# A graph-network layer on one core: the order of GpSimd's gathers written out by hand, in groups of 9, 9 and 6 behind points of TensorE

## The chip, the cores and the metric

The kernel runs on one core of a Trainium2 chip. The metric is device time in microseconds (us) of one execution. Before the change the median of three runs is 3001.91 us (3001.52 to 3004.13). A profiled execution, taken apart from these, took 2999.86 us; the span of its trace, from the first to the last instruction, is 2998.0 us.

The engines are named as the profile names them: PE is TensorE's matrix products and PEld its weight loads, DVE is VectorE, ACT is ScalarE, POOL is GpSimd, SP is SyncE, which only issues DMAs here.

## The reference

One layer of message passing over 12,500 nodes and 400,000 edges, which are sorted by their target `dst`. Each edge looks up the normalised features of its source and its target, passes a small two-layer network, and each node takes the maximum over the edges that end in it.

```python
h = jnp.maximum(_layernorm(x, axis=-1), 0.0)          # [12500, 32]
e_feat = jnp.concatenate([h[src], h[dst], edge_attr_32], axis=-1)
v = jax.nn.relu(e_feat @ W1 + b1) @ W2 + b2           # [400000, 96] -> 64 -> 32
x_cand = jax.ops.segment_max(v, dst, num_segments=num_nodes)
return x + jnp.maximum(x_cand, h[:, -32:])
```

## The kernel before

**Tiling.** The 400,000 edges are cut into four stripes, which lie side by side on 4 x 32 partitions. A stripe is walked in 196 chunks (`NCH`) of 512 edges (`C`), so a chunk is 4 x 512 edges. The main loop (L560) takes two chunks at a time: its counter c goes 0, 2, 4, and so on, and the iteration c finishes the chunks c and c + 1 and prepares the pair a = c + 2 and b = c + 3, for the most part.

**Where the source's features come from.** A chunk needs 16 columns (`K`) of 128 source rows. Twelve are fetched: GpSimd issues one indirect DMA for a column, 128 rows of 32 floats out of the table `h_d` in DRAM (`gather`, L153 to 162, the DMA itself at L159). Three columns (`SOME`) share one tile `gh`, here called a part: a chunk has 4 parts and a pair 8, that is 24 gathers. The parts are counted through from 0 for the pair 2, 3; the tile pool `gathered` has 18 buffers for them (L91). The other four columns (`MM`) are not fetched but multiplied out: `tile` (L245) has TensorE multiply a one-hot matrix `hot` with the table `hs` that lies in SBUF, 14 products of 128 x 448 into a PSUM bank `pv` (L256), and VectorE picks the row out of it (L260, L261). PSUM has three `pv` buffers, and other steps of the loop take them in turn too. The first two chunks have no such columns and are fetched from `x` itself (`raw_gather`, L168, 32 gathers in four calls `raw_gather(0)` to `(3)` with three buffers `xg`, so that the fourth waits for the first one's reader at L361); the last chunk has none either.

**From rows to features.** `to_features(c, part)` (L263) has VectorE transpose one part of `gh` into the chunk's tile `ht` (L274), or, with part = 4 (`J`), the result of `tile` (L277). VectorE works in order: the transposition of a part that has not landed holds up all that stands behind it.

**One iteration**, in TensorE's order: `into_ph` with `w1a` and the `ht` of the chunks c and c + 1 (16 products into four `ph` banks, L527), the transposition of the previous pair's result (`leave_1`, L500), `tile(a, 1)`, `edges_into(a)` (L527 with `ea`), the second layer (L586 into two `pv` banks), `windows_into(a)` (L527 with `qw`), `leave_2` (L511), and then a stretch of seven tiles without a break: `tile(a, 2)`, `tile(a, 3)`, `tile(b, 0)` to `tile(b, 3)`, `tile(a + 2, 0)`. VectorE follows with the same tiles' rows, with the parts between them (`to_features`), with its share of the one-hot matrices (L225) and with a scan (L594). In iteration c = 182 alone a check of the input stands behind `to_features(a + 2, 0)`: five small steps of VectorE and a product of TensorE at L637.

**Loads.** Every second iteration brings in four chunks' edge features, targets and penalties (`load`, L461): 1 MB through SP's queue and 1.5 MB through ScalarE's.

**What sets the order.** SP, PE, DVE and ACT run their instructions in the order of the source (`manual_schedule`, L180). GpSimd is left to the scheduler, which places the gathers that the source calls for in one go per chunk (L554 and L618). Its program: small constants, `raw_gather(0)` to `(2)`, the first ten gathers of `gh`, `raw_gather(3)`, the other 2,311 gathers, one addition (`again`, L621), which reuses the memory of the gathers' indices and so stands behind all of them. Its result is read in the last stage (L730). A gather waits for one made eight gathers before, and the first one of a part also for the reader of the buffer's last contents.

Of the kernel before, what the change touches and what calls it, by code (L numbers as in the profile page):

```python
# [11 lines left out]
BF16 = mybir.dt.bfloat16  # L12
I32 = mybir.dt.int32
AF = mybir.ActivationFunctionType
ALU = mybir.AluOpType
# [3 lines left out]
SP = mybir.EngineType.SP  # L19
PE = mybir.EngineType.PE  # L20
DVE = mybir.EngineType.DVE
ACT = mybir.EngineType.Activation

P = 128
N = 12500
E = 400000
D = 32
# [6 lines left out]
J = C // P  # L34
K = C // D
HALF = K // 2
NCH = 196
# [7 lines left out]
A0 = NT // A1  # L45
MM = 4
MMC = range(2, NCH - 1)
SOME = 3
# [3 lines left out]
FIRST = 16  # L52
PIECE = 2 * A0
GP = 3
ROUND = 12582912.0
LOW = 1e30
BY_ACT = range(A1 - 2, A1)
# [10 lines left out]
def gnn_kernel(ctx, tc, x, src, src_mm, src_t, dst, dst_ext, lo, lo_c, ends_b, edge_attr, weights, w1, w2, b2, out):  # L68
# [19 lines left out]
    nc = tc.nc  # L88
    const = ctx.enter_context(tc.tile_pool(name="const", bufs=1))
    dram = ctx.enter_context(tc.tile_pool(name="dram", bufs=1, space=DRAM))  # L90
    gathered = ctx.enter_context(tc.tile_pool(name="gathered", bufs=18))  # L91

    h_d = dram.tile([NP, D], F32, name="h_d")
    q_d = dram.tile([NP, HID], F32, name="q_d")
# [11 lines left out]
    pieces = [slice(k, min(k + PIECE, NT)) for k in range(0, NT, PIECE)]  # L106
    nc.scalar.dma_start(xs[:, pieces[GP]], x_v[:, pieces[GP]])
    for k in range(GP):
        (nc.sync, nc.scalar)[k % 2].dma_start(xs[:, pieces[k]], x_v[:, pieces[k]])
# [21 lines left out]
    hs = const.tile([P, 2, A1, D, A0], F32R, name="hs")  # L131
# [18 lines left out]
    general_i = const.tile([1, 1], I32, name="general_i")  # L150


    def gather(c):  # L153
        n = min(K - MM * (c in MMC), (SE - c * C) // D)
        parts = []
        for k in range(0, n, SOME):
            parts.append(gathered.tile([P, SOME, D], F32, name="gh"))
            for i in range(min(SOME, n - k)):
                nc.gpsimd.indirect_dma_start(  # L159
                    out=parts[-1][:, i, :], out_offset=None, in_=h_d[:, :],  # L160
                    in_offset=bass.IndirectOffsetOnAxis(ap=src_i[:, c, k + i:k + i + 1], axis=0))
        return parts


    early = ctx.enter_context(tc.tile_pool(name="early", bufs=2))
# [11 lines left out]
    for i in range(3):  # L177
        raw_gather(i)
    early_ps = ctx.enter_context(tc.tile_pool(name="early_ps", bufs=1, space=PSUM))
    ctx.enter_context(tc.manual_schedule(engines={SP, PE, DVE, ACT}))  # L180
    consts = early_ps.tile([P, C], F32, name="consts")[:, :W + A1 + A0]
    count_ps, key_ps, place_ps = consts[:, :W], consts[:, W:W + A1], consts[:, W + A1:]
    nc.vector.tensor_copy(consts, counts)
# [1 line left out]
    hots = {}  # L185
    masks = {}
    mm_rows = {}
    gh = {}
    hts = {}
    loaded_b, ats = {}, {}  # L190

    def group(out, of, last=None):

        nc.vector.tensor_scalar(out, of, 1.0 / A0, 0.5 / A0 - 0.5, op0=ALU.mult, op1=ALU.add)
        nc.vector.tensor_scalar(out, out, ROUND, None, op0=ALU.add)
        nc.vector.tensor_scalar(out if last is None else last, out, ROUND, None, op0=ALU.subtract)

# [22 lines left out]
    def one_hots(c, start, stop):  # L220

        if c not in MMC:
            return
        n = stop - start
        nc.vector.tensor_tensor(hot_of(c)[:, start:stop], keys[c][:, None, :].to_broadcast([P, n, MM * P]),  # L225
                                key_ps[:, start:stop, None].to_broadcast([P, n, MM * P]), op=ALU.is_equal)
# [15 lines left out]
                place_k[:, (c - MMC.start) * MM:(c - MMC.start + 1) * MM, None].to_broadcast([P, MM, A0]),  # L242
                op=ALU.is_equal)

    def tile(c, m):  # L245

        if c not in MMC:
            return
        if m == 0:
            mm_rows[c] = early.tile([P, MM, D], F32, name="gm", bufs=6)  # L250
        hot = hots[c]
        e = slice(m * P, (m + 1) * P)
        po = early_ps.tile([P, C], F32, name="pv", bufs=3)[:, :D * A0]
        for k in range(A1):
            for part in range(2):
                nc.tensor.matmul(po, hot[:, k, e], hs[:, part, k].rearrange("p f a -> p (f a)"),  # L256
                                 start=(k == 0 and part == 0), stop=(k == A1 - 1 and part == 1))
        of_group = po.rearrange("p (f a) -> p f a", a=A0)
        one = early.tile([P, D, A0], F32, name="one", bufs=2)
        nc.vector.tensor_tensor(one, of_group, masks[c][:, m, None, :].to_broadcast([P, D, A0]), op=ALU.mult)  # L260
        nc.vector.tensor_reduce(mm_rows[c][:, m, :], one, axis=AX.X, op=ALU.max)  # L261
# [42 lines left out]
    again = src_i.rearrange("p c t -> p (c t)").bitcast(F32).rearrange("p (t f) -> p t f", f=D)  # L304


    with tc.tile_pool(name="nodes", bufs=1) as pool, tc.tile_pool(name="nodes_ps", bufs=2, space=PSUM) as ps:
# [29 lines left out]
        def norm_3(st, h):  # L337

            n = h.shape[1]
            nc.vector.reciprocal(st[:, 1, :n], st[:, 0, :n])  # L340
            nc.vector.scalar_tensor_tensor(h, h, 0.0, st[:, 1, :n, None].to_broadcast([P, n, D]),
                                           op0=ALU.max, op1=ALU.mult)
# [11 lines left out]
        def raw_2(i):  # L354

            norm_2(raw_st[i], raw_sq[i])

        def raw_3(i):

            norm_3(raw_st[i], raws[i])  # L360
            nc.vector.transpose(raw_sq[i].rearrange("p k e -> p (k e)"),  # L361
                                raws[i].rearrange("p k f -> p (k f)"))

        for k in (0, 1, GP, 2):
            st, r = shares[k]
# [89 lines left out]
    with tc.tile_pool(name="edges", bufs=3) as pool, tc.tile_pool(name="edges_ps", bufs=1, space=PSUM) as ps:  # L455
# [27 lines left out]
        def window_hots(c):  # L483

            of = ofs[c] = pool.tile([P, C], F32, name="of", bufs=3)
            nc.scalar.activation(of, loaded[c][1], AF.Square, bias=below[:, c:c + 1])  # L486
            nc.scalar.activation(of, of, AF.Relu, bias=ones, scale=-1.0)  # L487
# [41 lines left out]
        def edges_into(c):  # L529

            if c < NCH:
                ph = [ps.tile([P, C], F32, name=f"ph{s}") for s in range(NS)]
                into_ph(ph, [(w1c, loaded[c + x][0]) for x in range(2)], True, False)
                return ph
# [15 lines left out]
        windows_into(0, ph)  # L550
        raw_2(3)
        raw_3(3)
        for k in range(2, 4):
            gh[k] = gather(k)  # L554
            window_hots(k)
        tile(2, 0)
        to_features(2, 0)
        sm = None
        sms = []
        for c in range(0, NCH, 2):  # L560
            a, b = c + 2, c + 3
# [18 lines left out]
            last = [lasts(c - 2 + x) for x in range(2)] if c else []  # L580
            ph = edges_into(a)
            pv = [early_ps.tile([P, C], F32, name="pv", bufs=3) for x in range(2)]
            for s in range(NS):
                for x in range(2):
                    g = slice(x * HID, (x + 1) * HID)
                    nc.tensor.matmul(pv[x][s * D:(s + 1) * D], w2x[g], hid[s][g], start=True, stop=True)  # L586
# [17 lines left out]
            tile(b, 0)  # L604
            to_features(b, 0)
            one_hots(a + 2, 0, 2)
            tile(b, 1)
            to_features(b, 1)
            one_hots(a + 2, 2, BY_ACT.start)
            mask_of(a + 2)  # L610
# [4 lines left out]
            if (c + 4) % BLOCK == 0 and (c + 4) // BLOCK < NB:  # L615
                make_block((c + 4) // BLOCK)
            for k in range(a + 2, min(a + 4, NCH)):
                gh[k] = gather(k)  # L618
                window_hots(k)
            if a + 2 == NCH - 2:  # L620
                nc.gpsimd.tensor_tensor(again.rearrange("p (g a) f -> p g a f", a=A0),  # L621
                                        hs[:, 0].rearrange("p g f a -> p g a f"),
                                        hs[:, 1].rearrange("p g f a -> p g a f"), op=ALU.add)
            tile(b, 3)
            to_features(b, 3)
            to_features(b, J)
            tile(a + 2, 0)
# [15 lines left out]
    with tc.tile_pool(name="out", bufs=1) as pool:  # L643
# [5 lines left out]
        with tc.If(flag > 0):  # L649
            with tc.tile_pool(name="general", bufs=1) as gp, tc.tile_pool(name="general_ps", bufs=1, space=PSUM) as ps:  # L650
# [16 lines left out]
                with tc.For_i(0, TS, 1) as i:  # L667
                    for s in range(NS):
# [42 lines left out]
                        old = gp.tile([P, D], F32, name="old")  # L711
# [84 lines left out]
```

## Time and profile before

| what | us |
|---|---|
| median of three runs | 3001.91 |
| profiled execution | 2999.86 |
| its span | 2998.0 |
| first and last start of a `gh` gather | 38.7, 2952.0 |
| first `ph` product of the main loop | 97.2 |
| last `ph` product | 2957.5 |
| last stage (L725 to L732) begins | 2977.9 |

The granted clock of TensorE is 0.98 as a mean over the span. The span is cut in 40 slices on the page; in the rows of digits a 9 means that an engine was busy 90% or more of a slice:

```profile
PE   2899999999999999999999999999999999999995
POOL 7777777777777777777777777777777777777774
```

The costliest groups of each of these two engines, with their busy time, the mean duration of one in ns, and the idle time before them with what ended it:

```profile
L256 PE MATMUL pv<-hs,hot 128*128 128x448 f32 x10808 | 2219.5, 364 | 0.9 <-DVE sm L594 0.9
L159 POOL DMA_INDIRECT gh<-h_d,src_i x2321 | 2195.5, 946 | 708.1 <-issue 529.2
```

A product's 364 ns are from its start to its end, and several are under way at once, so that the busy time is less than their sum. "issue" is idle time at whose end the profile shows nothing that was waited for. In the lines of a timeline the columns are the start in us, the duration, the engine, the line, the operation, the output and its inputs, how many such instructions are merged, and in brackets the idle time before and what ended it. In the table of waits they are the engine and the line that waited, what for, the us in total, how often, and the longest.

### The profile page before, as it was taken

Reading aid. Unit: us, or ns where it says so; the run is one execution under the profiler, and the core shown is the slowest. Engines: PE = TensorE matmul, PEld = TensorE weight load, DVE = VectorE, ACT = ScalarE, POOL = GpSimd, SP = SyncE. Lnnn points to the kernel's source line nnn. Section 1 sums busy time; section 2 is a strip of 40 time slices with the busy share of each in tenths; the row PEclk is TensorE's granted clock in tenths of the full one; section 3 lists DMA queues with packets and bytes.
Section 4 is the critical chain, followed back from the end, with each engine's and each line's share of the span. In section 5 each row is a group of like instructions: output and inputs, shape, how many; then the busy total and the mean of one; then the engine's idle time right before and its main releaser. Section 6 shows DMA issues by size and latency. Waiting matters only on the chain. (4 is left out here: it accounts for less than half of the span.)

```text
span 2998.0 us, 58325 instructions
## 1 busy us (share of the span) xinstructions
PE 2868.3 (96%) x21077; PEld 2312.6 (77%) x21077; DVE 2237.3 (75%) x3865; ACT 1068.6 (36%) x1693; POOL 2245.8 (75%) x2372
## 2 busy tenths in 40 slices
PE   2899999999999999999999999999999999999995
PEld 1678888788887877787777787778787878787774
DVE  5578778787787777777777777777777777777775
ACT  3333433333333333333333333333333333333331
POOL 7777777777777777777777777777777777777774
PEclk8899999999999999999999999999999999999997
DMA  6432233232233223222322232223222322232222
GB/s 201 134 76 67 70 81 75 64 81 73 71 76 79 70 60 87 70 71 60 83 70 71 59 89 69 67 63 81 73 71 59 83 75 67 63 81 74 67 54 73
DMA packets 189043, 229.40 MB, mean 77 GB/s; under 512 B 117821, under 2 KB 160461, under 8 KB 175950
## 3 DMA queue, kind: packets, MB, share of 16 engines
q10 hardware_dynamic: 26692, 110.28, 11.3%
q0 software_dynamic: 75296, 38.70, 10.3%
q1 hardware_dynamic: 86762, 76.66, 8.4%
q8 instruction: 165, 2.70, 0.4%
q14 instruction: 128, 1.05, 0.1%
HBM read 211.54 MB, written 13.85 MB: 75 GB/s over the span
## 5 line engine op out<-in xcount | busy, mean ns | idle before, releaser
L159 POOL DMA_INDIRECT gh<-h_d,src_i x2321 | 2195.5, 946 | 708.1 <-issue 529.2
L256 PE MATMUL pv<-hs,hot 128*128 128x448 f32 x10808 | 2219.5, 364 | 0.9 <-DVE sm L594 0.9
L256 PEld LDWEIGHTS pv<-hs,hot 128*128 128x128 f32 x10808 | 2016.7, 188 | 143.4 <-issue 3.2
L260 DVE TENSOR_TENSOR one<-pv,mask 128x448 f32<-128x448 f32 x772 | 477.5, 619 | 547.8 <-PE pv L256 543.9
L574 ACT ACTIVATE hid<-ph,wt 128x512 f32<-128x512 f32 x392 | 237.6, 689 | 1047.6 <-PE ph L527 825.4
L225 DVE TENSOR_TENSOR hot<-kb,consts 128x1024 fp32r<-128x1024 f16 (+2 forms) x385 | 559.2, 1452 | 0.0
L261 DVE TENSOR_REDUCE gm<-one 128x32 f32<-128x448 f32 x772 | 478.6, 620 | 26.6
L235 ACT ACTIVATE hot<-away,ones 128x512 fp32r<-128x512 f32 x386 | 279.4, 724 | 488.2 <-issue 472.5
L274 DVE STREAM_TRANSPOSE ht<-gh 128x96 f32<-128x96 f32 x774 | 208.2, 269 | 109.4 <-DMA gh<-h_d,src_i 109.4
L234 ACT ACTIVATE away<-kb,key_n 128x512 f32<-128x512 f16 x386 | 276.6, 716 | 0.0
L594 DVE TENSOR_TENSOR_SCAN sm<-pb,sm,pv 128x512 f32<-128x512 bf16 x195 | 247.5, 1269 | 11.1 <-PE pv L586 0.5
L527 PE MATMUL ph<-ht,wt 32*64 32x512 f32 x1568 | 142.1, 640 | 25.1 <-DVE ht L277 25.1
L511 PEld LDWEIGHTS pv<-so,last 128*64 128x64 f32 x3136 | 100.1, 138 | 80.4 <-PE pv L586 74.7
L500 PEld LDWEIGHTS pv<-ident,sm 128*128 128x128 f32 x784 | 89.5, 147 | 85.3 <-issue 70.8
L486 ACT ACTIVATE of<-db,below 128x512 f32<-128x512 int32 x196 | 138.8, 708 | 31.6 <-DMA db<-in_dst_ext 27.0
L487 ACT ACTIVATE of<-of,ones 128x512 f32<-128x512 f32 x196 | 142.1, 725 | 6.4
L527 PE MATMUL ph<-of,qw 32*64 32x512 f32 x1568 | 114.0, 617 | 21.0 <-DMA qw<-q_d 21.0
L515 ACT ACTIVATE wo<-pv 128x128 f32<-128x128 f32 x98 | 27.3, 278 | 298.1 <-PE pv L511 286.5
L527 PE MATMUL ph<-ea,wt 32*64 32x512 f32 x1568 | 110.1, 617 | 21.7 <-DMA qw<-q_d 21.7
L502 DVE TENSOR_TENSOR so<-pv,wt 128x512 f32<-128x512 f32 x196 | 125.2, 676 | 3.9 <-PE pv L500 3.9
L492 DVE TENSOR_TENSOR last<-consts,at 128x512 f32<-128x512 f32 x196 | 122.5, 663 | 0.0
L511 PE MATMUL pv<-so,last 128*64 128x64 f32 x3136 | 113.7, 226 | 1.4 <-DVE last L492 1.4
(80 smaller groups left out, 611.8 us busy)
## 6 DMA issues: line engine op xcount, KB each, us to landing
ea<-in_edge_attr SPq DMA_DIRECT2D x49, 1024.0 KB
db<-in_dst_ext ACTq DMA_DIRECT2D x48, 1024.0 KB
gh<-h_d,src_i POOLq DMA_INDIRECT x2321
pb<-pen_d ACTq DMA_DIRECT2D x48, 512.0 KB
kb<-key_d ACTq DMA_DIRECT2D x47, 512.0 KB
qw<-q_d SPq DMA_DIRECT2D x784, 8.0 KB
top_d<-wo SPq DMA_DIRECT2D x784, 4.0 KB
top_d<-zero ACTq DMA_DIRECT2D x2, 1568.0 KB
```

The lines of the kernel that those rows point to most:

```text
L159: nc.gpsimd.indirect_dma_start(out=parts[-1][:, i, :], out_offset=None, in_=h_d[:, :], in_offset=bass.IndirectOffsetOnAxis(ap=src_i[:, c, ...
L225: nc.vector.tensor_tensor(hot_of(c)[:, start:stop], keys[c][:, None, :].to_broadcast([P, n, MM * P]), key_ps[:, start:stop, None].to_broad ...
L234: nc.scalar.activation(away, keys[c], AF.Square, bias=key_n[:, k:k + 1])
L235: nc.scalar.activation(hot_of(c)[:, k], away, AF.Relu, bias=ones, scale=-1.0)
L256: nc.tensor.matmul(po, hot[:, k, e], hs[:, part, k].rearrange("p f a -> p (f a)"), start=(k == 0 and part == 0), stop=(k == A1 - 1 and par ...
L260: nc.vector.tensor_tensor(one, of_group, masks[c][:, m, None, :].to_broadcast([P, D, A0]), op=ALU.mult)
L261: nc.vector.tensor_reduce(mm_rows[c][:, m, :], one, axis=AX.X, op=ALU.max)
L274: nc.vector.transpose(ht[:, r].rearrange("p k e -> p (k e)"), gh[c][part][:, :r.stop - r.start].rearrange("p k f -> p (k f)"))
L511: nc.tensor.matmul(pw[g * 2 * W:(g + 1) * 2 * W, x * 2 * D:(x + 1) * 2 * D], last[x][:, j, 2 * g:2 * g + 2].rearrange("p s w -> p (s w)"), ...
L527: nc.tensor.matmul(ph[s][x * HID:(x + 1) * HID], w[g], e[g], start=start, stop=stop)
L574: nc.scalar.activation(hid[s], ph[s], AF.Relu, bias=b1c)
L594: nc.vector.tensor_tensor_scan(sm, loaded.pop(c + x)[2], pv[x], before, op0=ALU.add, op1=ALU.max)
```

## The change

GpSimd is added to the engines whose order is that of the source. `gather` takes a range of parts, and `gather_group(a, g)` issues three of a pair's eight parts, the next three or the last two: 9, 9 and 6 gathers. The groups are called for at three places of the iteration: behind the allocation of the two `pv` banks of the second layer (group 1 of the pair a), behind `tile(b, 1)` (group 2) and behind `tile(b, 3)` (group 0 of the pair a + 2). Ahead of each, `hold` adds one product to TensorE: its weights and its single column are the upper halves of the floats of the part that lies 18 places back from the next one (`old`), and its result goes into a corner of a PSUM bank that the next real product overwrites. The result is used nowhere; the product makes TensorE a reader of that part. `hold` does nothing until 18 parts have been called for. The addition into `again` is called for one iteration later than before, again behind the last gathers.

```diff
--- before.py
+++ after.py
@@ -20,6 +20,7 @@
 PE = mybir.EngineType.PE
 DVE = mybir.EngineType.DVE
 ACT = mybir.EngineType.Activation
+POOL = mybir.EngineType.Pool
 
 P = 128
 N = 12500
@@ -52,6 +53,8 @@
 FIRST = 16
 PIECE = 2 * A0
 GP = 3
+RING = 18
+GROUPS = (0, 3, 6, 2 * J)
 ROUND = 12582912.0
 LOW = 1e30
 BY_ACT = range(A1 - 2, A1)
@@ -88,7 +91,7 @@
     nc = tc.nc
     const = ctx.enter_context(tc.tile_pool(name="const", bufs=1))
     dram = ctx.enter_context(tc.tile_pool(name="dram", bufs=1, space=DRAM))
-    gathered = ctx.enter_context(tc.tile_pool(name="gathered", bufs=18))
+    gathered = ctx.enter_context(tc.tile_pool(name="gathered", bufs=RING))
 
     h_d = dram.tile([NP, D], F32, name="h_d")
     q_d = dram.tile([NP, HID], F32, name="q_d")
@@ -150,16 +153,34 @@
     general_i = const.tile([1, 1], I32, name="general_i")
 
 
-    def gather(c):
+    all_parts = []
+    gh = {}
+
+    def gather(c, first, stop):
+
         n = min(K - MM * (c in MMC), (SE - c * C) // D)
-        parts = []
-        for k in range(0, n, SOME):
+        parts = gh.setdefault(c, [])
+        for k in list(range(0, n, SOME))[first:stop]:
             parts.append(gathered.tile([P, SOME, D], F32, name="gh"))
+            all_parts.append(parts[-1])
             for i in range(min(SOME, n - k)):
                 nc.gpsimd.indirect_dma_start(
                     out=parts[-1][:, i, :], out_offset=None, in_=h_d[:, :],
                     in_offset=bass.IndirectOffsetOnAxis(ap=src_i[:, c, k + i:k + i + 1], axis=0))
-        return parts
+
+    def gather_group(a, g):
+
+        first, stop = GROUPS[g], GROUPS[g + 1]
+        for x in range(2):
+            if a + x < NCH:
+                gather(a + x, max(first - J * x, 0), max(stop - J * x, 0) if x == 0 or stop < 2 * J else None)
+
+    def hold(bank):
+
+        if len(all_parts) >= RING:
+            old = all_parts[len(all_parts) - RING].rearrange("p k f -> p (k f)").bitcast(BF16)
+            old = old.rearrange("p (k two) -> p k two", two=2)[:, :, 1]
+            nc.tensor.matmul(bank[:SOME * D, 0:1], old, old[:, 0:1], start=True, stop=True)
 
 
     early = ctx.enter_context(tc.tile_pool(name="early", bufs=2))
@@ -177,7 +198,7 @@
     for i in range(3):
         raw_gather(i)
     early_ps = ctx.enter_context(tc.tile_pool(name="early_ps", bufs=1, space=PSUM))
-    ctx.enter_context(tc.manual_schedule(engines={SP, PE, DVE, ACT}))
+    ctx.enter_context(tc.manual_schedule(engines={SP, PE, DVE, ACT, POOL}))
     consts = early_ps.tile([P, C], F32, name="consts")[:, :W + A1 + A0]
     count_ps, key_ps, place_ps = consts[:, :W], consts[:, W:W + A1], consts[:, W + A1:]
     nc.vector.tensor_copy(consts, counts)
@@ -185,7 +206,6 @@
     hots = {}
     masks = {}
     mm_rows = {}
-    gh = {}
     hts = {}
     loaded_b, ats = {}, {}
 
@@ -242,7 +262,7 @@
                 place_k[:, (c - MMC.start) * MM:(c - MMC.start + 1) * MM, None].to_broadcast([P, MM, A0]),
                 op=ALU.is_equal)
 
-    def tile(c, m):
+    def tile(c, m, held=False):
 
         if c not in MMC:
             return
@@ -251,6 +271,8 @@
         hot = hots[c]
         e = slice(m * P, (m + 1) * P)
         po = early_ps.tile([P, C], F32, name="pv", bufs=3)[:, :D * A0]
+        if held:
+            hold(po)
         for k in range(A1):
             for part in range(2):
                 nc.tensor.matmul(po, hot[:, k, e], hs[:, part, k].rearrange("p f a -> p (f a)"),
@@ -550,8 +572,8 @@
         windows_into(0, ph)
         raw_2(3)
         raw_3(3)
+        gather_group(2, 0)
         for k in range(2, 4):
-            gh[k] = gather(k)
             window_hots(k)
         tile(2, 0)
         to_features(2, 0)
@@ -580,6 +602,8 @@
             last = [lasts(c - 2 + x) for x in range(2)] if c else []
             ph = edges_into(a)
             pv = [early_ps.tile([P, C], F32, name="pv", bufs=3) for x in range(2)]
+            hold(pv[0])
+            gather_group(a, 1)
             for s in range(NS):
                 for x in range(2):
                     g = slice(x * HID, (x + 1) * HID)
@@ -604,7 +628,12 @@
             tile(b, 0)
             to_features(b, 0)
             one_hots(a + 2, 0, 2)
-            tile(b, 1)
+            tile(b, 1, held=True)
+            gather_group(a, 2)
+            if a == NCH - 2:
+                nc.gpsimd.tensor_tensor(again.rearrange("p (g a) f -> p g a f", a=A0),
+                                        hs[:, 0].rearrange("p g f a -> p g a f"),
+                                        hs[:, 1].rearrange("p g f a -> p g a f"), op=ALU.add)
             to_features(b, 1)
             one_hots(a + 2, 2, BY_ACT.start)
             mask_of(a + 2)
@@ -615,13 +644,9 @@
             if (c + 4) % BLOCK == 0 and (c + 4) // BLOCK < NB:
                 make_block((c + 4) // BLOCK)
             for k in range(a + 2, min(a + 4, NCH)):
-                gh[k] = gather(k)
                 window_hots(k)
-            if a + 2 == NCH - 2:
-                nc.gpsimd.tensor_tensor(again.rearrange("p (g a) f -> p g a f", a=A0),
-                                        hs[:, 0].rearrange("p g f a -> p g a f"),
-                                        hs[:, 1].rearrange("p g f a -> p g a f"), op=ALU.add)
-            tile(b, 3)
+            tile(b, 3, held=True)
+            gather_group(a + 2, 0)
             to_features(b, 3)
             to_features(b, J)
             tile(a + 2, 0)
```

## The prediction

> **What bounds the kernel now.** I read the busy times first, and they mislead: TensorE shows 96%, GpSimd 75%.
>
> ```profile
> PE 2868.3 (96%) x21077; PEld 2312.6 (77%) x21077; DVE 2237.3 (75%) x3865; ACT 1068.6 (36%) x1693; POOL 2245.8 (75%) x2372
> ```
>
> Then the waits over all engines, for GpSimd's gathers and for whoever waits for them:
>
> ```profile
> POOL gh L159 <- issue: 529.2, 1736, 0.4
> ...
> DVE ht L274 <- DMA gh<-h_d,src_i: 109.4, 60, 4.4
> ```
>
> The longest gap before any gather is 0.4 us: GpSimd is never held up. Each gather takes 0.945 us and 0.30 us to get going. The timeline of GpSimd shows this pitch at gathers 11 and 12 and at the last one:
>
> ```profile
> 62.47 0.94 POOL L159 DMA_INDIRECT gh<-h_d,src_i  x1 [0.31 <-issue]
> 63.72 0.95 POOL L159 DMA_INDIRECT gh<-h_d,src_i  x1 [0.30 <-issue]
> ...
> 2951.97 0.95 POOL L159 DMA_INDIRECT gh<-h_d,src_i  x1 [0.30 <-DMA gh<-h_d,src_i]
> ```
>
> From the 11th to the 2321st: (2951.97 - 62.47) / 2310 = 1.2509 us. A pair of chunks has 24 gathers, so it costs GpSimd 30.02 us. TensorE needs less for a pair when nothing is late, as its timeline early on shows by the start of the last product into `ph`:
>
> ```profile
> 124.13 1.11 PE L527 MATMUL ph<-ht,wt 32*64 32x512 f32 x16
> ...
> 153.01 1.11 PE L527 MATMUL ph<-ht,wt 32*64 32x512 f32 x16
> ...
> 181.89 1.11 PE L527 MATMUL ph<-ht,wt 32*64 32x512 f32 x16
> ```
>
> 28.88 us from one to the next. So GpSimd starts ahead and loses 1.14 us a pair. The windows show when it has lost its lead (PE and POOL busy us; up to 1060 us PE has no gap at all, afterwards it has, while POOL goes on alike):
>
> ```profile
> 600.00:1060.00 460.00, 460.00 (x3446) 375.13 (x3445) 358.97 (x622) 171.58 (x272) 347.87 (x368) 1.00 0.30 74
> 1060.00:1560.00 500.00, 493.06 (x3569) 398.79 (x3568) 376.38 (x657) 176.58 (x280) 378.05 (x401) 0.99 0.30 73
> ```
>
> All 60 waits of VectorE for a gather lie behind 1060 us. The last is in the iteration c = 182, and there it stops TensorE through the product at L637, which stands behind it:
>
> ```profile
> 2822.62 0.28 DVE L274 STREAM_TRANSPOSE ht<-gh 128x96 f32<-128x96 f32 x1 [2.11 <-DMA gh<-h_d,src_i]
> ...
> 2823.56 0.19 PE L637 MATMUL pv<-ones,worst 128*1 128x1 f32 x2 [6.58 <-DVE worst L635]
> ```
>
> From 2823.7 us to the last `ph` at 2957.5 TensorE runs at its own pace, then 40.5 us of tail to 2998.0. So the end = GpSimd's 2211th gather (part 736 by count of three-gather tiles, from 0) + its landing + TensorE's pace. A delay of GpSimd before that point comes out in full; TensorE time added before it is hidden as long as GpSimd stays the slower one.
>
> In the Trainium skill, Perfetto Trace Analysis, section Identifying the Most-Contended Engine, matmul busy time is called a poor measure and GpSimd is to be ranked by its occupancy. The trace agrees on the first (96% with slack) and not on the second: 75% here is an engine with no slack, because the 0.30 us between gathers are not counted as busy.
>
> **The change, part by part.**
>
> *Same work on GpSimd.* 2321 gathers, 32 raw gathers, one addition: nothing is removed. The last eight raw gathers move ahead of the first ten `gh` gathers; their buffer's last reader (L361) ends at 32.48 us, before GpSimd gets to either at 38.67, so 18 gathers in another order end at 62.4 as now. Bounds: the first raw gathers took up to 1.47 us instead of 0.945, so +-1 us; I take 0. The addition (11.5 us) still stands last on GpSimd; it ended at 2966.4, its reader L730 starts at 2984.4.
>
> *The holds.* `hold` has TensorE read the tile from 18 parts back. That makes TensorE its last reader, and the built order shows what follows: the slot is not the next to be handed out. Ten slots freed earlier go first. The first gather that waits for TensorE is the 88th (part 29), not the 58th (part 19) that follows the first hold in the source, and this shift of ten parts stays to the end. The other parts now wait for VectorE's transposition of a part 17, soon 12 back instead of 18, since six slots lie idle with the holds. So GpSimd may lead by 12 parts, 45 us.
>
> Against before's timeline: part 29 starts at 158.74, its TensorE point (the products of L586 in c = 4) is at 158.93: 0.2 us. Part 30 starts at 162.48; part 18, whose slot it gets, is transposed at 166.39 + 0.27 = 166.66: 4.2 us. Part 38 would wait 3.1, 46 1.9, 54 1.6, 62 0.6, from 70 on none, and by 600 us the gates are open over 10 us early. The waits do not add: whoever waited 4.2 us at part 30 is late enough for the others. With one hold's 0.15 us ahead of part 18: **4.3 us**. Behind the waiting gather stand all later ones; VectorE waits for them only after 1060 us, but there it pays the 4.3. Bounds: 0 (if TensorE's main loop starts 4 us sooner) to 6 (starts 2 us later).
>
> *What a hold costs TensorE.* 284 of them: a weight load 128x96 and a product of one column, bf16. No such row exists. From below: the smallest product (L511, 32 in 1.08 us) has a pitch of 0.034 us with its load. From above: the load (128x64: 138 ns) and the reload of the broken tile stream (L256 LDWEIGHTS: 188 ns) in the open: 0.33. I take **0.15**, the nearest row: a tile entered from another kind of product (L500) takes 183.78 to 186.77 = 2.99 us, one in the stream 19.81 / 7 = 2.83. Their waits for the old tile's DMA are long met. Until 2823.7 GpSimd covers it: 3 x 0.15 = 0.45 us a pair against 1.14 to spare. Behind it 14 holds remain (three in each of c = 184 to 190, one each in 192 and 194): 14 x 0.15 = **2.1 us**; by the bounds 0.5 to 4.6.
>
> The Trainium skill, TensorE: Matmul & The Clock Gate, section Back-to-back issue gap, puts the floor of a product with few columns at about 25 ns; by that the last term would be 0.4 us instead of 2.1. No row here shows a one-column product in a stream.
>
> Sum: 2998.0 + 4.3 + 2.1 = 3004.4 span, + 1.9 around it = 3006.3 us against 2999.9 of the profiled execution. The median of the runs is 2.05 higher, 3001.9; so **3008**, +0.2%. 0.2% (6.0 us) is about what a measurement of this kernel can tell from no change.
>
> **Rivals.**
>
> *The last late gather lands sooner: not slower.* Part 736 was transposed 7.2 us after GpSimd had finished it, since it lands amid the 2.5 MB of loads issued at 2805 to 2808. The other waits for a part at this place of the pair had 5.3 to 7.6. If 4 us of shift against the loads bring it to 5.3, 1.9 are given back: 3006. It decides when the lead at that wait is under 6.7 us. For it: the spread. Against: in this stretch the loads follow TensorE, which shifts too.
>
> *Holds dear enough to make TensorE the bound.* Without late gathers TensorE alone would end at 2924.9: 124.13 (the second `ph`) + 95 x 28.88 + 16.7 (the short last pair) + 40.5 of tail. It takes over when 284 holds cost 3002.3 - 2924.9 = 77.4 us, 0.27 each. At 0.33: 3018, 3022 as a run; if each also drains the product (L511's 226 ns), 0.55: 3085. For it: two of three holds break the densest stream. Against: L511's pitch.
>
> *TensorE is the bound already.* Its 96% speak for it; then every hold counts from the first pair on, 284 x 0.15 = 43 us: 3045, and at 0.034 each 3012. Against: GpSimd's even pitch in all windows, and the 60 waits for gathers. The skill's ranking by occupancy, named above, would put GpSimd behind TensorE's weight loads (77%) and so lead to this rival.
>
> *The holds bind the group they stand before.* The 58th gather would start at 158.93, and the 2211th end 2154 x 1.2509 us later, at 2853.4 instead of 2815.4: +38, 3042 with the rest. Against it: the built order.
>
> **How the numbers follow.** Forecast 0.40 (3005 to 3013; of it 0.28 over the 0.2% bound), sooner landing 0.25 (0.02 over), dear holds 0.12, TensorE bound 0.05, holds as named 0.08, something not seen 0.10 (0.08 of it faster). Slower: 0.28 + 0.02 + 0.12 + 0.05 + 0.08 + 0.02 = 0.57; same 0.12 + 0.23 = 0.35; faster 0.08. The range 3001 to 3036 leaves out the holds as named, the upper part of dear holds and the unseen gain.
>
> **What would show it.** Right: gathers at 1.25 us, one or a few waits of GpSimd adding up to about 4 us between 150 and 270 us and none later; the last gather ending near 2957; 28.88 + 0.45 us a pair early on; VectorE's waits for gathers again about 60, starting later than 1060 us. Wrong: waits of GpSimd for TensorE past 600 us (holds as named); no waits for gathers and a pair over 30.02 us (dear holds); a pitch of gathers other than 1.251 would break everything above.

## The result and the profile after

| | kernel before | changed kernel |
|---|---|---|
| median of 14 runs each, us | 3003.86 (3001.52 to 3007.11) | 3011.70 (3008.73 to 3013.67) |
| profiled execution: its time, us | 2999.86 | 3009.26 |
| its span, us | 2998.0 | 3007.5 |

The ratio is 1.0023, with a 95% interval of 1.0015 to 1.0031: slower, by just more than the 0.2% that can be told from nothing. The forecast was 3008 us, against a median before that has itself come out 2 us higher than in the first three runs.

The shares of busy time say as little as before. From the page of the changed kernel:

```profile
PE 2892.5 (96%) x21361; PEld 2327.9 (77%) x21361; DVE 2237.0 (74%) x3865; ACT 1068.4 (36%) x1693; POOL 2247.8 (75%) x2372
```

The waits of the changed kernel (us in total, times, longest) show what is new and what stayed:

```profile
POOL gh L167 <- issue: 553.0, 1803, 2.9
...
DVE ht L296 <- DMA gh<-h_d,src_i: 91.5, 58, 3.4
...
POOL gh L167 <- DVE ht L296: 10.8, 28, 2.6
...
POOL gh L167 <- PE pv L183: 0.9, 3, 0.3
```

GpSimd, which had a single gap over 0.4 us before (0.78 us at the 1354th gather), now has waits of 2.9 and 2.6 us. Of the holds at L183, which the change sets as its gates, only 0.9 us of waits are named, none longer than the 0.3 us that stand before any gather. VectorE still waits for gathers, 58 times. Where the two long waits are, the timeline of GpSimd shows (start, duration, then in brackets the idle time before the instruction and what ended it):

```profile
150.12 0.95 POOL L167 DMA_INDIRECT gh<-h_d,src_i  x1 [0.30 <-issue]
153.97 0.96 POOL L167 DMA_INDIRECT gh<-h_d,src_i  x1 [2.90 <-issue]
...
163.98 0.94 POOL L167 DMA_INDIRECT gh<-h_d,src_i  x1 [0.30 <-issue]
167.51 0.94 POOL L167 DMA_INDIRECT gh<-h_d,src_i  x1 [2.59 <-DVE ht L296]
...
2959.94 0.94 POOL L167 DMA_INDIRECT gh<-h_d,src_i  x1 [0.30 <-DMA gh<-h_d,src_i]
```

They are the 82nd and the 91st gather, that is the first of part 27 and of part 30. The 91st stood at 162.48 before, so it is 5.03 us late. The last gather stood at 2951.97 and is 7.97 us late.

TensorE's timeline in the same kernel shows its own pair, and the holds in it:

```profile
153.46 1.11 PE L549 MATMUL ph<-ht,wt 32*64 32x512 f32 x16
...
159.38 0.21 PE L183 MATMUL pv<-gh 128*96 128x1 bf16 x1
159.52 1.09 PE L610 MATMUL pv<-hid,wt 64*32 64x512 f32 x16
...
171.19 0.17 PE L183 MATMUL pv<-gh 128*96 128x1 bf16 x1
171.21 5.86 PE L278 MATMUL pv<-hs,hot 128*128 128x448 f32 x28
...
182.72 1.11 PE L549 MATMUL ph<-ht,wt 32*64 32x512 f32 x16
...
211.98 1.11 PE L549 MATMUL ph<-ht,wt 32*64 32x512 f32 x16
```

From one `ph` to the next 29.26 us instead of 28.88: 0.38 us for three holds, 0.127 each. The windows (PE, PEld, DVE, ACT, POOL busy us) show that TensorE keeps a gapless stretch until 1060 us and has next to no gap until 1560, where it had 7 us before:

```profile
600.00:1060.00 460.00, 460.00 (x3435) 375.59 (x3428) 353.58 (x613) 166.43 (x264) 348.02 (x368) 1.00 0.30 74
1060.00:1560.00 500.00, 499.14 (x3718) 404.01 (x3718) 382.16 (x664) 182.25 (x289) 377.90 (x400) 1.00 0.30 72
```

TensorE's pair has become 0.38 us longer, so GpSimd needs longer to lose its lead; GpSimd's busy time in the two windows is the same as before (347.87 and 378.05). The end of the kernel in three lines, VectorE's and TensorE's timelines around the last late gather and TensorE's last `ph`:

```profile
2828.88 0.28 DVE L296 STREAM_TRANSPOSE ht<-gh 128x96 f32<-128x96 f32 x1 [1.12 <-DMA gh<-h_d,src_i]
...
2829.86 0.19 PE L662 MATMUL pv<-ones,worst 128*1 128x1 f32 x2 [3.43 <-DVE worst L660]
...
2965.47 1.78 PE L549 MATMUL ph<-ht,wt 32*64 32x512 f32 x16 [1.75 <-DVE ht L299]
```

With that the 9.5 us between the two spans can be followed from place to place:

| place | before | after | late by | what came on top |
|---|---|---|---|---|
| 11th gather starts | 62.47 | 62.54 | 0.1 | |
| 91st gather starts | 162.48 | 167.51 | 5.0 | the two waits |
| 2211th gather (end of part 736) starts | 2814.44 | 2822.31 | 7.9 | a pitch of 1.2522 instead of 1.2509 us |
| part 736 is transposed | 2822.62 | 2828.88 | 6.3 | it has landed 1.6 us sooner after its gather |
| product of the check (L637, now L662) | 2823.56 | 2829.86 | 6.3 | |
| last `ph` | 2957.50 | 2965.47 | 8.0 | 1.7: the 14 holds behind |
| end | 2998.0 | 3007.5 | 9.5 | 1.5 in the tail |

The waits and the holds, 6.7 us together, were forecast (6.4). The pitch, the sooner landing and the tail were not in that sum; whether they belong to the change is one question for the experiments.

### The profile page after: what moved, and what is told of

Read it like the earlier page. It is cut to its first block, busy times and chain, and to the rows that moved or that the text cites. A ratio compares the mean times of both kernels' runs of the same rounds, so it can differ in the third digit from the quotient of the medians.

```text
span 3007.5 us, 59180 instructions
## 1 busy us (share of the span) xinstructions
PE 2892.5 (96%) x21361; PEld 2327.9 (77%) x21361; DVE 2237.0 (74%) x3865; ACT 1068.4 (36%) x1693; POOL 2247.8 (75%) x2372
## 5 line engine op out<-in xcount | busy, mean ns | idle before, releaser
L549 PE MATMUL ph<-ht,wt 32*64 32x512 f32 x1568 | 134.6, 626 | 11.7 <-DVE ht L299 11.4
```

The source lines that it names most:

```text
L549: nc.tensor.matmul(ph[s][x * HID:(x + 1) * HID], w[g], e[g], start=start, stop=stop)
```

## The experiments

The first four ran on one chip, on which the kernel before has a median of 2996.38 us, the next four on another with 2996.24. So the numbers of an expectation, which start from 3003.9, are to be read as differences to the kernel before; the measured ones are given so.

### The order by hand without the holds

```diff
     def hold(bank):
-        if len(all_parts) >= RING:
+        if False:
```

> The changed kernel with GpSimd's order by hand, but no product in the holds. Theory (what costs is the 5.0 us for which GpSimd waits twice for a slot at 154 and 167 us, since the holds hand the slots back late, and some 1.7 us for the 14 last holds; the order by itself costs nothing): every part gets the slot of the part 18 back, no gap of GpSimd over 1 us near 154 or 167 us, pair at 28.88 us while TensorE sets the pace, median 3002 to 3006 like the kernel before. Rival A (the order by itself costs: the raw gathers moved ahead, and a pitch of 1.2522 instead of 1.2509 us over 2230 gathers, 2.9 us): pitch 1.252, median 3007 to 3009. Rival B (the order by itself makes all of it): 3010 to 3013.

2995.46 us, ratio 0.9996 (0.9987 to 1.0005): the same as the kernel before. GpSimd's timeline at the two places:

```profile
151.66 0.95 POOL L167 DMA_INDIRECT gh<-h_d,src_i  x1 [0.30 <-issue]
152.92 0.94 POOL L167 DMA_INDIRECT gh<-h_d,src_i  x1 [0.30 <-issue]
...
161.66 0.95 POOL L167 DMA_INDIRECT gh<-h_d,src_i  x1 [0.30 <-issue]
162.92 0.95 POOL L167 DMA_INDIRECT gh<-h_d,src_i  x1 [0.30 <-issue]
```

Both waits are gone. So GpSimd's order by hand, with the raw gathers ahead, costs nothing that can be seen (by the interval 1.5 us at most), and what the change costs comes with the products in the holds. The pitch from the 91st gather to the last is 1.2493 us: rival A falls too.

### Fewer slots, no holds

```diff
-    gathered = ctx.enter_context(tc.tile_pool(name="gathered", bufs=RING))
+    gathered = ctx.enter_context(tc.tile_pool(name="gathered", bufs=12))
...
-        if len(all_parts) >= RING:
+        if False:
```

> The same without products in the holds, but with 12 slots for gathered parts instead of 18: every part gets the slot of the part 12 back, the look-ahead that the holds leave. Theory (GpSimd is the bound from its first gather on, and what it loses early is lost at the end): by the transpositions in the changed kernel's trace GpSimd waits 5.6 us for part 12, 0.3 for part 13 and 2.4 for part 14, and never after: 8.3 us, so 3010 to 3014 (the median before 3003.9 plus 8.3, and 1.6 less if the last late gather lands sooner). Rival (TensorE sets the end, a GpSimd late by 8 us catches up): 3002 to 3005. Rival (12 slots bind again and again later): waits past 200 us, over 3016.

3004.60 us, ratio 1.0029 (1.0017 to 1.0040), 8.2 us more. GpSimd's timeline has the waits at the parts 12, 13 and 14, and one at the 82nd gather:

```profile
99.93 0.94 POOL L167 DMA_INDIRECT gh<-h_d,src_i  x1 [4.72 <-DVE ht L296]
...
104.15 0.94 POOL L167 DMA_INDIRECT gh<-h_d,src_i  x1 [0.78 <-DVE ht L296]
...
110.27 0.94 POOL L167 DMA_INDIRECT gh<-h_d,src_i  x1 [2.67 <-DVE ht L296]
...
159.86 0.95 POOL L167 DMA_INDIRECT gh<-h_d,src_i  x1 [1.20 <-DVE one L282]
```

Less the 0.30 us before any gather these are 4.4, 0.5, 2.4 and 0.9: 8.2 us within the first 160 us, and 8.2 us at the end of 3000. Only the first three, 7.3 us together, are waits for a slot; the slot of the 82nd gather (part 15's) had been free since 152.87 us, so the 8.3 us of the expectation were met in part by luck. So is the agreement to the tenth: against order_alone, from which this kernel differs in the slots alone, the medians differ by 9.1 us and the two spans by 7.2. No hold is in this kernel. This shows the main step: what GpSimd loses early is not made up, although TensorE does not notice for another 900 us.

### All holds, more slots

```diff
-    gathered = ctx.enter_context(tc.tile_pool(name="gathered", bufs=RING))
+    gathered = ctx.enter_context(tc.tile_pool(name="gathered", bufs=RING + 6))
```

> The changed kernel with all its 284 holds, but 24 slots for gathered parts, so that parts wait for a transposition 18 back again. Theory: the two waits at 154 and 167 us (5.0 us) are gone; the holds stay hidden behind GpSimd until about 2830 us, and the last 14 of them stay: median 3004 to 3008, pair 29.26 us early on, the end of the last gather about 5 us sooner than in the changed kernel. Rival (the holds as such slow the kernel through TensorE, 0.13 us each in part or in full): no less than the changed kernel, 3010 to 3013.

3000.28 us, 3.9 more than the kernel before, ratio 1.0010 (1.0001 to 1.0019): about half of what the change costs is gone. GpSimd's timeline:

```profile
150.71 0.94 POOL L167 DMA_INDIRECT gh<-h_d,src_i  x1 [0.30 <-issue]
153.14 0.95 POOL L167 DMA_INDIRECT gh<-h_d,src_i  x1 [1.49 <-DVE gm L283]
...
163.13 0.94 POOL L167 DMA_INDIRECT gh<-h_d,src_i  x1 [0.30 <-issue]
164.38 0.95 POOL L167 DMA_INDIRECT gh<-h_d,src_i  x1 [0.30 <-issue]
```

The wait at part 30 has gone with the shortage of slots. At the 82nd gather 1.2 us remain, in a kernel in which that gather's slot has been free for long (even part 10, 17 parts back, is transposed by 136.4 us). The VectorE record that the profile names there ended 0.11 us before the gather; at every wait for a slot shown here the gather starts 0.27 us behind the end of the transposition. So the long wait at 153.97 us in the changed kernel was only in part a wait for a slot: part 15, 12 parts back, was transposed until 152.22, and the gather started 1.74 us later. no_late_holds, holds_x2 and holds_x4 have the same 1.74 us there, that is 1.47 more than at other slots.

### Without the last holds

```diff
-        if len(all_parts) >= RING:
+        if RING <= len(all_parts) < 740:
```

> The changed kernel without the last 17 or so holds (those behind the last late gather at about 2829 us). Theory: the early waits stay (5.0 us), TensorE saves 14 x 0.12 = 1.7 us behind 2829 us: median 3009 to 3011 against 3011.7 of the changed kernel; from the product of the flag to the last product into ph 133.9 us instead of 135.6. Rival (the tail is set by GpSimd's last gathers and not by TensorE): no change, 135.6 again.

3002.77 us, ratio 1.0020 (1.0010 to 1.0030), against 1.0023 for the changed kernel. The interval is too wide to see 1.7 us in the times. In TensorE's timeline it can be seen:

```profile
2824.68 0.19 PE L662 MATMUL pv<-ones,worst 128*1 128x1 f32 x2 [5.96 <-DVE worst L660]
...
2958.66 1.78 PE L549 MATMUL ph<-ht,wt 32*64 32x512 f32 x16 [1.75 <-DVE ht L299]
```

133.98 us from the one to the other. (The flag is the result of the check that L637, now L662, takes part in.) The same stretch in all kernels where that product waited for a late gather: 133.9 (before), 134.5, 134.1 (the two without holds) and 134.0 here, with one hold behind it; 135.6 (after and ring_24) with 14. The 14 holds cost 1.5 us. Pair by pair it is steadier: the first pair behind the check takes between 30.5 and 31.1 us in these kernels, then three pairs take 28.88 us each without and 29.26 with holds, and the short last one 16.70 and 16.84.

### Two and four products in a hold

```diff
-            nc.tensor.matmul(bank[:SOME * D, 0:1], old, old[:, 0:1], start=True, stop=True)
+            for _ in range(2):
+                nc.tensor.matmul(bank[:SOME * D, 0:1], old, old[:, 0:1], start=True, stop=True)
```

> The changed kernel with two products in each hold instead of one. Theory (hidden until a hold costs some 0.27 us): pair 29.64 us early, still under GpSimd's 29.97 on this chip, so only the gate at part 30 (4 holds ahead of it, 0.5 us) and the last 14 holds (1.6 us) come on top of the changed kernel: 1.0023 x 2996.4 = 3003.3, plus 2.1, so 3004 to 3008. Rival (holds count in full): 36 us more, 3039.

3006.20 us, ratio 1.0035 (1.0021 to 1.0050), 10.0 us more than before. TensorE's timeline, and the wait of VectorE for gathers:

```profile
181.65 1.11 PE L550 MATMUL ph<-ht,wt 32*64 32x512 f32 x16
...
187.58 0.25 PE L184 MATMUL pv<-gh 128*96 128x1 bf16 x2
187.76 1.09 PE L611 MATMUL pv<-hid,wt 64*32 64x512 f32 x16
...
211.05 1.11 PE L550 MATMUL ph<-ht,wt 32*64 32x512 f32 x16
```

```profile
DVE ht L297 <- DMA gh<-h_d,src_i: 58.4, 38, 2.7
```

284 more products, and the kernel is 2 to 4 us slower than the changed one (10.0 us over the kernel before against 7.8 by the medians, 1.0035 against 1.0023 by the ratios, whose intervals overlap), not 36. The pair is 29.40 us, 0.14 more than with single products, not the 0.38 that I had put in: the second product of a hold costs 0.047 us, the first 0.127. VectorE waits 38 times for gathers, no longer 58: the slack is being used up, but is there.

With `range(4)`:

> The changed kernel with four products in each hold. Theory: if each costs the same 0.127 us the pair is 30.40 us, over GpSimd's 29.97; TensorE takes over, VectorE waits for no gathers and the kernel ends at 2926.8 + 284 x 4 x 0.127 = 3071. If the second to fourth cost only the 0.034 us of the smallest product's pitch, a hold is 0.23, the pair 29.57, and it stays hidden: 3004 to 3009. The early pair tells which; between 0.27 and 0.30 us a hold both engines bind. Rival (holds count in full from the first): three times 36 us more than the changed kernel even if hidden, 3111.

3005.28 us, ratio 1.0030 (1.0019 to 1.0041). TensorE's timeline and the windows:

```profile
184.86 1.11 PE L550 MATMUL ph<-ht,wt 32*64 32x512 f32 x16
...
190.78 0.34 PE L184 MATMUL pv<-gh 128*96 128x1 bf16 x4
...
214.52 1.11 PE L550 MATMUL ph<-ht,wt 32*64 32x512 f32 x16
```

```profile
1060.00:1560.00 500.00, 500.00 (x3857) 407.31 (x3856) 381.71 (x664) 182.03 (x289) 378.05 (x401) 1.00 0.29 70
2000.00:2500.00 500.00, 500.00 (x3854) 407.72 (x3838) 378.49 (x656) 178.31 (x283) 377.76 (x402) 1.00 0.30 72
```

Now the pair is 29.66 us, 0.78 over the one without holds: 0.26 us for each place with four products. TensorE has no gap over 0.3 us from the second `ph` to the check, and VectorE's waits for gathers are gone from the list. So TensorE has just become the bound, and the time is still that of holds_x2.

### What TensorE needs alone

To see a hold in the open, GpSimd was given less to do. In the chunks 2 to 194 the twelfth gathered column is not fetched, and a copy of the tenth stands in its place; 193 gathers are gone.

```diff
-            for i in range(min(SOME, n - k)):
+            for i in range(min(SOME, n - k) - (c in MMC and k + SOME >= n)):
...
+            short = c in MMC and r.stop == n
             if r.start < n:
+                r = slice(r.start, r.stop - short)
                 nc.vector.transpose(ht[:, r].rearrange("p k e -> p (k e)"),
                                     gh[c][part][:, :r.stop - r.start].rearrange("p k f -> p (k f)"))
+            if short:
+                nc.vector.transpose(ht[:, r.stop], gh[c][part][:, 0])
```

Without the products in the holds:

> Like order_alone (no products in the holds), and the chunks 2 to 194 gather eleven columns instead of twelve; the twelfth column of each is left out and a copy of its tenth stands there (one small transposition more on VectorE for each), so 193 gathers, 241 us of GpSimd, are gone. Theory (GpSimd is the bound, TensorE alone would need 28.88 us a pair and end at 2924.9 us of span): TensorE takes over, pair 28.88 us all the way, no waits of VectorE for gathers, 2922 to 2935 as a run. Rival (TensorE is the bound already): no change against order_alone, 2995.

2935.21 us, ratio 0.9793 (0.9776 to 0.9809). With them:

> The changed kernel with all its holds and the same eleven columns (the twelfth left out as in eleven_free). Theory: with GpSimd no longer slower, every hold counts in full: 284 x 0.127 = 36 us over eleven_free, 2958 to 2971, pair 29.26 us all the way. Rival (a product of one column costs some 0.03 us in a stream and the 0.38 us a pair comes from something else early on): under 2945.

2968.34 us, ratio 0.9908 (0.9892 to 0.9925). TensorE's timeline and window of the first and then of the second:

```profile
2006.36 1.11 PE L553 MATMUL ph<-ht,wt 32*64 32x512 f32 x16
...
2035.24 1.11 PE L553 MATMUL ph<-ht,wt 32*64 32x512 f32 x16
```

```profile
2000.00:2500.00 500.00, 500.00 (x3730) 408.11 (x3729) 391.99 (x715) 183.28 (x291) 359.97 (x381) 1.00 0.29 73
```

```profile
2025.24 1.11 PE L553 MATMUL ph<-ht,wt 32*64 32x512 f32 x16
...
2054.50 1.11 PE L553 MATMUL ph<-ht,wt 32*64 32x512 f32 x16
```

```profile
2000.00:2500.00 500.00, 500.00 (x3753) 405.62 (x3759) 385.13 (x698) 184.48 (x293) 355.20 (x377) 1.00 0.29 72
```

241 us taken off GpSimd bring 61: TensorE takes over, without a gap in the window, at 28.88 us a pair. Now the holds count in full: 33.1 us between the medians for 284, 0.117 each, and 29.26 us a pair at 2000 us as at 200. The same 284 products that cost 33 us of TensorE's time here cost 1.5 us of it in the changed kernel, in which GpSimd hides all but 14; the slots that they keep come on top there.

### Four runs on another chip

The last four ran on a chip on which the kernel before itself took 4223 us (4169 to 4248), at a granted clock of 0.88 instead of 0.98, and their times say nothing on what is asked here: GpSimd waits 1244 us for VectorE's transpositions there in the kernel before, so it is not the bound. Two details of their traces do bear on it. The line of clocks for the kernel before there, once more profiled:

```profile
core 0: 4227.6 us, clock 0.883
```

The kernel before once more:

> The kernel before once more, for a profile of its own from the same chip as the others. Theory (GpSimd's pitch of 1.2509 against 1.2522 us in the first two profiles belongs to the chip and the execution, not to the change): pitch as in the other runs of this call to 0.001 us, ratio 1.000. And the time from the last product into ph to the end, 39.3 us in its first profile and 40.8 in the changed kernel's: 39 to 40 again if the difference belongs to the change, anywhere between 39 and 41 if it is chance.

4215.14 us, ratio 1.0014 (0.9968 to 1.0061). The changed kernel once more:

> The changed kernel once more. Theory: the same two waits, gather 91 about 5 us late against the kernel before; 14 holds behind the last late gather cost 1.5 us; ratio 1.002 to 1.003; pitch of the gathers from the 91st on as in the kernel before to 0.001 us. Rival (the change makes each gather 0.0013 us slower): the pitch is higher than in the kernel before by that much again, 2.9 us over the run.

4180.53 us, ratio 0.9921 (0.9891 to 0.9951); why it is ahead there stays open. The two details: the median time from one gather's start to the next is 1.249 us in both kernels on this chip, so the change does not make a gather slower. And from the start of the last product into `ph` to the end it is 39.5 us in the kernel before and 40.7 in the changed one, as 39.3 and 40.8 in the first two profiles: by the mark that the expectation set, this difference belongs to the change. With 24 slots and without the last holds:

```diff
-    gathered = ctx.enter_context(tc.tile_pool(name="gathered", bufs=RING))
+    gathered = ctx.enter_context(tc.tile_pool(name="gathered", bufs=RING + 6))
...
-        if len(all_parts) >= RING:
+        if RING <= len(all_parts) < 740:
```

> The changed kernel with 24 slots and without the last 13 holds: both of what the theory charges to the change is taken away, 271 holds stay. Theory: 271 holds hidden, so within 0.1% of the kernel before, but for the gap of some 1.2 us at gather 82 that runs with holds have shown even where no slot is late; 0 to 3 us. Rival (ring_24 is 3.9 us slower than before because of something the holds do all along, not of the last 14): still 3 to 4 us slower.

4212.52 us, ratio 0.9978 (0.9943 to 1.0012). And a kernel that the others had pointed to, with twelve of GpSimd's gathers given to TensorE (the fifth tile has its own one-hot matrix and mask, and 15 slots instead of 18 make room for them):

```diff
+FIVE = range(61, 181, 10)
...
-        n = min(K - MM * (c in MMC), (SE - c * C) // D)
+        n = min(K - MM * (c in MMC) - (c in FIVE), (SE - c * C) // D)
...
             tile(b, 3)
+            if b in FIVE:
+                tile(b, MM)
```

> The kernel before, but in 12 chunks (61 to 171, each tenth) the twelfth gathered column is made by TensorE as a fifth tile of products; 15 slots for gathered parts instead of 18, to make room. Theory (GpSimd is the bound by some 60 us over TensorE): 12 gathers less are 12 x 1.249 = 15.0 us less at the last late gather, and the 12 x 2.9 us on TensorE are hidden: 2981 where the kernel before takes 2996 (ratio 0.995). Rival (TensorE is the bound): 35 us slower. Rival (VectorE, which gets some 2.6 us more in each of those chunks, or the 15 slots, holds it up): ratio 0.997 to 1.002.

4212.70 us, ratio 0.9996 (0.9962 to 1.0030). On that chip GpSimd waits 1231 us for slots in this kernel, and fewer gathers cannot help it. Whether it wins on a chip like the first two stays open.

## Why the prediction was right, and where not

**What bounds the kernel: right.** Some 8 us lost by GpSimd early, without any hold, come out as 7 to 9 us at the end (slots_12), 284 more products on TensorE as 2 to 4 (holds_x2). The share of busy time, by which TensorE with 96% would be the bound, would have had both the other way round. Two readings on the way were off, with no effect on the sum: one gap of 0.78 us does stand before a gather (the 1354th), where 0.4 was called the longest, and raw gathers took up to 1.82 us, not 1.47.

**TensorE alone: 11 us too early.** I had it end at 2924.9 us of span; eleven_free ends at 2935.8. From the second `ph` to the last but one its pairs take 28.957 us on average, not 28.88, since now and then one is longer: 95 x 0.077 = 7.3 us. The rest is the start, 2.4 us later, and the tail, 1.0 longer. So the point where TensorE takes over lies at (3002.3 - 2935.8) / 284 = 0.23 us a hold, not 0.27 (the two spans are from two chips). Four products in a hold, at 0.26, are just past it, as their windows show.

**The early waits: the place and the rule right, 5.0 us instead of 4.3.** Part 30 waited for the transposition of part 18, as worked out; the holds' own gate at part 29 cost nothing that shows. Of the 0.7 us missing, 0.45 is the start of the main loop, which came that much later in this execution (second `ph` at 124.58 instead of 124.13), and 0.27 is the time from the end of a transposition (167.24) to the start of the gather (167.51), which I had left out. One wait I had not listed: part 27, whose slot is that of part 15, transposed until 152.22, so that its gather could not start before about 152.5 instead of 151.4. It does not add, nor do the 1.47 us that came on top of it there, since the wait for part 18 ends at the same time whatever came before it. ring_24, which gives the slots back, takes the wait at part 30 away, and order_alone both.

**A hold: 0.15 forecast, 0.127 measured** (0.117 by the times of eleven_holds and eleven_free). Behind the last late gather 14 of them cost 1.5 us instead of 2.1. That all others are hidden, eleven_holds shows from the other side. The floor of 25 ns that the Trainium skill gives (TensorE: Matmul & The Clock Gate, section Back-to-back issue gap) would have made it 0.4 us, as an estimate. The trace has 127 ns for the first such product, which enters from another kind of product and leaves into a third, and 47 ns for the next one directly behind it: the floor was not reached in either place.

**What the sum left out.** The sum gave +6.4 us, the medians differ by 7.8, the two spans by 9.5. Three things that were not in it stand in the table of the result:
- The pitch, +2.9 us. It does not belong to the change: from the 91st gather to the last it is 1.2493 without holds (order_alone) and 1.2493 with them (no_late_holds, holds_x2) on chips where other executions ran; ring_24 has 1.2498, slots_12 1.2496. The step that took 1.2509 for a constant of the kernel was wrong by 0.0013 upwards and 0.0016 downwards, which over 2230 gathers is 2.9 and 3.6 us, against 7.8 for the whole change.
- The landing of part 736, -1.6 us. This is the rival with the sooner landing, and by its own mark (a lead under 6.7 us at the last wait; it is 5.6) it came true in this execution. But its reason, the shift against the loads, did not hold: with no shift the lead is 6.8 (order_alone) and 5.5 (ring_24, 1.2 us late), with the largest 6.5 (slots_12), and 7.0 in no_late_holds. It varies by a microsecond up and down from trace to trace.
- The tail, +1.5 us. From the last `ph` to the end it takes 40.0 to 40.9 us in before, order_alone and slots_12, 41.9 to 42.3 in after, ring_24, no_late_holds and holds_x2, but 40.5 in holds_x4; eleven_free has 41.6, eleven_holds 42.9. The traces narrow it down. From the end of ScalarE's last `wo` to the first load of the last stage it takes 7.4 to 7.9 us in the four kernels without holds and 9.0 to 9.7 in those with holds, holds_x4 (7.5) apart. In after, ring_24, no_late_holds and eleven_holds one of SP's last issues of `top_d<-wo` takes 1.64, 1.48, 1.46 and 1.36 us where its neighbours take 0.3; in the four without holds none of these last issues does. The second profile of the changed kernel has it too (1.57), that of the kernel before does not. So this looks like a cost of the changed program and not like chance. But why such an issue is long no row shows; holds_x2 (0.58) and holds_x4 (none) do not fit, and five_12, which has no holds, has one as well (1.18): open.

**Dear holds: ruled out** by 0.127, and shown where they would begin by holds_x4. **TensorE as the bound already: ruled out** by slots_12 and holds_x2. **Holds that bind as named: ruled out**; past 600 us no wait of GpSimd for TensorE is longer than the usual 0.3 us.

So the forecast of +0.2% was right for its reasons in the main, the waits for slots and the last holds. That it came so near is in part luck: the pitch and the landing, +2.9 and -1.6 us, cancelled in part, and the tail had no term. ring_24 takes the waits for slots away and leaves +3.9 us. Its span is 3.8 over that of order_alone: 1.2 at the 82nd gather, 1.0 from the check to the last `ph` (the last holds), 1.4 in the tail; what remains, 0.3 at the start, 1.2 of pitch and -1.3 of landing, is of the size that differs from trace to trace.

## What to carry to other kernels

For an engine that issues many small instructions, count them and multiply by the pitch from start to start; its share of busy time leaves out what lies between. If this product is the span, every wait of that engine costs in full wherever it stands, even where no one waits for it for another 900 us, and time on the others is free until their own sum comes near. And a second reader added to a ring of buffers can take slots away, however short it is: it hands them back when it comes to run. Here it kept six, and six more slots took the wait at part 30 away.

## What the runs showed of the hardware

**Gaps at the same gathers in one kernel after the other.** GpSimd has gaps that no slot explains, and most stand at the same places by count: at the 82nd gather (after 1.5 us, ring_24 1.2, slots_12 0.9), the 506th (ring_24 0.5, holds_x2 0.4, no_late_holds 0.3) and the 1354th (before 0.5, after 0.8, order_alone 0.8, ring_24 0.7, slots_12 0.9), that is 424 and 848 apart. A few stand elsewhere (slots_12 at the 824th, 0.8; holds_x4 at the 1460th, 0.9). They come in some executions and not in others. Where the profile names a VectorE record as what ended one, this had ended between 0.04 and 0.6 us before the gather, at another distance each time, and not the 0.27 us of a wait for a slot. By the Trainium skill (Runtime: NRT & Kernel Launch, section Instruction fetch mechanics) an engine's instructions are fetched in blocks, which is said to be mostly hidden. No run here shows that these gaps are such fetches; of the transfers that the traces list as instruction, none falls into the gap at the 82nd gather in after, ring_24, slots_12, no_late_holds, holds_x2 or holds_x4.

**The same product costs 127 ns alone and 47 ns behind its like.** With one, two and four products of 128 x 1 in a place, the pair of chunks grows by 0.38, 0.52 and 0.78 us over three places. So most of the price of a small product among others seems to be the change from one kind to the other; that the change itself is what costs was not shown apart.

**A chip can run the same kernel at 4223 us.** With a mean granted clock of 0.88 instead of 0.98 that is 41% more time, where the clock alone would make 11%.
